# Three score banks, two woven sets of value banks, and two quarters moved into the last group of a two-layer decoder kernel

## The chip, the cores and the metric

The kernel runs on one core of a Trainium2 chip. The metric is the device time of one execution in microseconds; smaller is better. The core has TensorE (PE in the profile, its weight loads PEld), VectorE (DVE), ScalarE (ACT), GpSimd (POOL) and SyncE (SP), which issues nearly all DMAs. Matmul results go to PSUM, which has eight banks of 128 x 512 fp32 values; a bank can be written again when VectorE or ScalarE has read what was in it ("evicted" it).

## The reference

Two post-norm decoder layers over x of 4 x 256 tokens by 512, all in fp32: a latent attention with 32 heads, a gated feed-forward with integer weights, a causal attention with 32 heads, and a linear layer with soft-weighted low-rank experts.

```python
x = layernorm(x + L0_attn(x))
x = layernorm(x + L0_ffn(x))
x = layernorm(x + L1_attn(x))
x = layernorm(x + L1_ffn(x))

def L0_attn(h):                      # 32 heads, no mask
    q_c = h @ Wq_c.T + bq_c          # 192 wide
    q = (q_c @ Wq_up.T + bq_up)      # per head 128 + 64
    kv = h @ Wkv_c.T + bkv_c         # 64 latent + 64 shared key
    kvu = kv[..., :64] @ Wkv_up.T + bkv_up
    k = concat(kvu[..., :128], kv[..., 64:]);  v = kvu[..., 128:]
    o = softmax(q @ k.T / sqrt(192)) @ v
    return sum over heads of o @ Wo.T, + bo

def L1_attn(h):                      # 32 heads of 128, causal
    q = h @ wq;  k, v = split(h @ wkv)
    return softmax(mask(q @ k.T * 192 ** -0.5)) @ v @ wo
```

## The kernel before

The kernel is one program under a tile framework. The source gives instructions in an order, and a scheduler of the framework sets the order on each engine from it: an instruction may be put ahead of others of its engine. Each engine then works through its own list strictly in order and waits on semaphores. A `bank(tag)` is a PSUM tile of the pool that is open; the pool gives each tag so many banks, and a tile of a tag waits until the tile before it in the same bank has been read.

Stages, in order of time:

1. Projections and folding (0 to 56 us). `fold` folds key weights into query weights, in banks of the tag o.
2. The first attention (56 to 441 us), `NP` = 16 pairs of heads by `B` = 4 batches: 64 units. A unit computes the scores of two heads (`scores0`, L63 with output ps_s, one bank for each head), the maxima (L344), a bias (L348, L350), four exps on ScalarE (L355), the normalization (L364, L370 on VectorE, L368 on ScalarE), transposes (L379), their copies to SBUF (L383, one on each of VectorE and ScalarE), and the output (L396, bank o, copied by ScalarE, L400). In the loop the scores of a unit stand ahead of the transposes and the output of the unit before. Between them stand the queries of the next pair (`q_units`: `upper` L294, `lower` L302, evicted by ScalarE in L306) and, every other pair, a value product (`value_unit`), summed into `oacc` by VectorE (L409). GpSimd prepares weights of the second attention meanwhile (`prepare`, L136 to L139), which SP writes to DRAM.
3. The output projection: for each of eight token tiles a matmul with `wo0` in a bank p, VectorE's addition to x (L476), a layernorm, four transposes and a copy into `xT` (L128). A layernorm has two forms: by VectorE (L112 to L121, ScalarE does the square root) or, with `scalar`, by ScalarE with short VectorE steps between (L96 to L109).
4. The feed-forward (461 to 668 us), with products in the seven-product scheme (each 2 x 2 block product is made of seven products and sums of them). Its last loop does layernorm and transposes too.
5. The second attention. The eight groups of four heads (`NG`, `GH`) get queries and keys, and pairs of groups their values, by the seven-product scheme twice, an outer and an inner one. `seven` returns seven units of work; a unit is a product into one of three banks b0, b1, b2 and its eviction: by ScalarE (L792) or by VectorE as a sum (L795). The fifth and the last product go to the same bank.
   - The value stage (668 to 853 us): 28 stages of seven units, one after another in the order of `vorder`. Each stage asks for the weights of the third one behind it (`Stored.get`, DMAs qb and qc). After the first stage `input_blocks2` transposes the last two token tiles and makes combinations of the input on VectorE (`xcomb` L764, `blocks2` L523 to L526) and GpSimd; later stages need them.
   - Queries and keys of group 0 (853 to 880 us), then for each group 16 iterations of attention (four heads by four batches: `scores1` L63, L1084, L1088, L1092; `softmax1` L1104; `transposes1` L1110, L1112; `output1` L1119, L1120, written to DRAM as attd by SP). Between the parts of an iteration stand units of the next group's queries and keys, spread evenly by weight (`todo`). These consist of four stages each; the last, p = 3, has one inner product for each unit instead of two, and its result is added to heads 2 and 3 of the group (L879 on GpSimd). Partial products of stages with p = 1 and 3 lie in x[4:8], those of p = 2 in x[0:4], while x itself is in DRAM (`xd`).
   - In the last group's iterations there are no further queries; the units are those of the output projection of groups 0 and 1 (`stages_o`, L1043, 1052), and `lead` = 4 holds them back from the first and the last iterations. For them, behind the first iteration, SP loads attd (`o_load`, 2 MB each, into the buffers of old values and of old input combinations), the weights and x.
6. The output projection of groups 2 to 7 (1478 to 1616 us), and the expert layer (to 1706 us).

SP handles its list in order; a load that waits holds back those behind it. The end of each iteration's attention is written from three buffers `att`.

## Time and profile before

| | us |
|---|---|
| three timed runs | 1712.03, 1713.04 (median), 1717.1 |
| profiled execution | 1707.83 |
| its span, first to last instruction | 1706.0 |
| mean granted clock of TensorE | 0.998 |

| stage | from, to (us) | busy TensorE, VectorE, ScalarE, GpSimd |
|---|---|---|
| first attention, first units | 56, 126 | 70.0, 48.9, 42.9, 61.4 |
| first attention, the rest | 126, 438 | 300.2, 224.2, 195.3, 214.2 |
| its end and the projection | 438, 472 | 31.7, 24.5, 19.8, 13.2 |
| value stage, first four stages | 668, 702 | 28.9, 25.5, 6.1, 29.4 |
| value stage, the rest | 702, 853 | 150.6, 102.5, 28.7, 106.3 |
| second attention to its last group | 880, 1393 | 513.0, 358.3, 282.4, 375.2 |
| the last group's beginning | 1393, 1426 | 27.8, 23.8, 13.6, 28.3 |

Some records of matmuls are missing from a trace (some per cent), so that a small gap in TensorE's busy time need not be a wait; the waits by name and the distance from one start to the next tell more. A line such as `308.54 0.70 PE L63 MATMUL ps_s<-kT,qh ... x2` gives the start, the length, the engine, the line of the source, output and inputs, and how many records are merged. An fp32 matmul of the source is two records. In square brackets stands idle time of the engine before the row and what ended it.

### The profile page before, as it was taken

How to read it: one execution, taken by the hardware profiler on the slowest of the kernel's cores; microseconds unless marked ns; L12 is line 12 of the kernel's file. 1: busy time of each engine (PE TensorE's matmuls, PEld its weight loads, DVE VectorE, ACT ScalarE, POOL GpSimd, SP SyncE). 2: the span in 40 equal slices, each digit the busy share in tenths (PEclk: the TensorE clock that was granted, in tenths of full speed). 3: DMA queues.
4: the chain of work that ended last, by engine and by line, in shares of the span. 5: the costliest groups of instructions: out<-in, count | busy, mean ns of one | idle time of the engine just before them, and what ended most of it. 6: DMA issues, size and time to landing. Idle time of an engine off the chain costs nothing.

```text
span 1706.0 us, 24182 instructions
## 1 busy us (share of the span) xinstructions
PE 1662.6 (97%) x7954; PEld 1292.4 (76%) x7954; DVE 1066.8 (63%) x2351; ACT 701.4 (41%) x2066; POOL 1106.5 (65%) x1330
## 2 busy tenths in 40 slices
PE   8999999999999999999999999999999999999998
PEld 5566656666488888788878888888888878888854
DVE  3567777776754546676677666766667676433454
ACT  1566666656622101111115555555555562300043
POOL 1988878880236462876668668687686767689530
PEclk9999999999999999999999999999999999999999
DMA  9455555450222002567633233253332344443000
GB/s 339 152 208 202 205 216 209 174 190 36 69 70 73 27 25 72 179 228 246 205 97 123 102 110 135 75 178 113 100 134 75 117 160 171 158 149 116 33 19 31
DMA packets 96252, 226.90 MB, mean 133 GB/s; under 512 B 10272, under 2 KB 53792, under 8 KB 90112
## 3 DMA queue, kind: packets, MB, share of 16 engines
q1 hardware_dynamic: 94464, 224.54, 38.3%
q8 instruction: 64, 1.05, 0.3%
q10 hardware_dynamic: 1664, 0.81, 0.2%
q14 instruction: 60, 0.49, 0.1%
HBM read 140.38 MB, written 84.93 MB: 132 GB/s over the span
## 4 chain that ended last, share of the span: by engine, by line
PE 83%; DVE 10%; ACT 5%; issue 1%; DMA 1%; POOL 0%; DVEq 0%; ACTq 0%; POOLq 0%
PE ps_b L858 20%; PE ps_b L1043 11%; PE ps_b L953 10%; PE ps_s L63 9%; PE ps_o L1119 4%; ACT pr L355 3%; PE ps_s L604 3%; PE ps_p L294 3%; PE ps_o L63 2%; PE ps_p L63 2%; PE ps_t L1110 2%; PE ps_o L604 2%; PE ps_p L604 2%; PE ps_o L396 2%; DVE nmx L344 2%; DVE pr L370 2%
## 5 line engine op out<-in xcount | busy, mean ns | idle before, releaser
L1092 ACT ACTIVATE pr<-ps_s,nmx 128x128 f32<-128x128 f32 (+1 forms) x256 | 105.3, 418 | 106.2 <-DVE nmx L1088 106.2
L63 PE MATMUL ps_s<-kT,qh 128*128 128x256 f32 x512 | 130.5, 392 | 5.0 <-ACT pr L355 4.8
L1052 DVE TENSOR_TENSOR x<-ps_b,x 128x512 f32<-128x512 f32 x96 | 66.0, 690 | 108.5 <-PE ps_b L1043 101.2
L355 ACT ACTIVATE pr<-ps_s,ebias 128x256 f32<-128x256 f32 x256 | 117.9, 473 | 32.8 <-DVE ebias L350 30.8
L1104 ACT ACTIVATE pr<-pr,rc 128x128 f32<-128x128 f32 (+1 forms) x256 | 103.6, 448 | 61.3 <-DVE rc L1102 59.3
L63 PEld LDWEIGHTS ps_s<-kT,qh 128*128 128x128 f32 x512 | 90.9, 189 | 48.8 <-ACT pr L355 29.4
L1084 DVE TENSOR_TENSOR ps_s<-ps_s,mask 128x256 f32<-128x256 f32 x128 | 55.3, 432 | 108.3 <-PE ps_s L63 108.3
L795 DVE SCALAR_TENSOR_TENSOR x<-ps_b,p 128x512 f32<-128x512 f32 (+1 forms) x174 | 106.7, 614 | 25.1 <-PE ps_b L858 14.8
L792 ACT ACTIVATE p<-ps_b 128x512 f32<-128x512 f32 x92 | 51.5, 560 | 132.5 <-PE ps_b L953 76.0
L344 DVE TENSOR_REDUCE nmx<-ps_s 128x2 f32<-128x512 f32 x128 | 86.4, 686 | 27.4 <-PE ps_s L63 26.6
L136 POOL TENSOR_TENSOR ws<-ws 128x128 f32<-128x128 f32 (+1 forms) x128 | 70.7, 569 | 46.4 <-DMA ws<-in_wq 26.0
L370 DVE TENSOR_SCALAR pr<-pr,rc 128x256 f32<-128x256 f32 x192 | 93.4, 513 | 4.3
L1062 POOL TENSOR_TENSOR x<-x,po 128x512 f32<-128x512 f32 x48 | 60.1, 1271 | 38.1 <-DVE x L1052 29.6
L795 DVE SCALAR_TENSOR_TENSOR x<-ps_b,x 128x512 f32<-128x512 f32 (+1 forms) x116 | 71.1, 613 | 21.1 <-PE ps_b L953 12.1
L1119 PE MATMUL ps_o<-pT,v 128*128 128x256 f32 x256 | 82.9, 406 | 0.3 <-DVE pT L1112 0.2
L1088 DVE TENSOR_REDUCE nmx<-ps_s 128x1 f32<-128x128 f32 (+1 forms) x256 | 79.3, 351 | 3.7
L383 ACT COPY pT<-ps_t 128x512 f32<-128x512 f32 x64 | 37.5, 587 | 105.3 <-PE ps_t L379 105.3
L1112 DVE COPY pT<-ps_t 128x384 f32<-128x384 f32 x128 | 70.3, 550 | 11.5 <-PE ps_t L1110 11.5
L379 PE MATMUL ps_t<-ident,pr 128*128 128x128 f32 x512 | 70.0, 274 | 3.3 <-DVE pr L370 2.1
L139 POOL TENSOR_TENSOR ws<-ws,ws 128x128 f32<-128x128 f32 (+1 forms) x128 | 70.6, 566 | 2.4
L137 POOL TENSOR_TENSOR ws<-ws 128x128 f32<-128x128 f32 (+1 forms) x128 | 71.0, 571 | 1.3
L138 POOL TENSOR_TENSOR ws<-ws 128x128 f32<-128x128 f32 (+1 forms) x128 | 70.8, 567 | 1.3
(663 smaller groups left out, 4599.4 us busy)
## 6 DMA issues: line engine op xcount, KB each, us to landing
attd<-att SPq DMA_DIRECT2D x128, 128.0 KB, 1.8
vw<-ws SPq DMA_DIRECT2D x56, 256.0 KB, 2.4
qd<-ws SPq DMA_DIRECT2D x56, 256.0 KB, 2.3
qb<-vw SPq DMA_DIRECT2D x28, 512.0 KB, 4.6
qb<-qd SPq DMA_DIRECT2D x24, 512.0 KB, 4.5
v<-vd SPq DMA_DIRECT2D x6, 2048.0 KB, 8.6
qc<-vw SPq DMA_DIRECT2D x28, 384.0 KB, 4.1
vw<-ws SPq DMA_DIRECT2D x24, 384.0 KB, 2.4
```

What stands on the lines that cost most here:

```text
L63: nc.tensor.matmul(o, l, r, start=(i == 0), stop=(i == len(pairs) - 1))
L344: nc.vector.tensor_reduce(nmx[:, i, :], sc, AX.X, ALU.max, negate=True)
L355: nc.scalar.activation(pr[:, i, qt, :], sc[:, qt, :], AF.Exp, bias=bias[:, i, qt:qt + 1], accum_out=sm[:, i, qt:qt + 1],)
L370: nc.vector.tensor_scalar(prs, prs, rc[:, i, qt:qt + 1], None, ALU.mult)
L604: nc.tensor.matmul(banks_of[tag], lhs[i][:, k, :], rhs[i][:, k, :], start=first and k == 0, stop=k == 1, skip_group_check=True,)
L795: nc.vector.scalar_tensor_tensor(o[key], acc, scale, o[other], ALU.mult, ALU.add)
L858: nc.tensor.matmul(acc[:, e, :], pr.inner[i][k], inner[i][k], start=first and e == 0, stop=True, skip_group_check=True,)
L953: nc.tensor.matmul(acc[:, t, :].rearrange("p (h c) -> p h c", h=2), inner[i][k][:, t * P:(t + 1) * P], pr.inner[i][k], start=first and t = ...
L1043: nc.tensor.matmul(st[tag][:, tt, :], box["left"][i][:, k, (t0 + tt) * P:(t0 + tt + 1) * P], box["right"][i][:, k, :], start=first and tt ...
L1092: nc.scalar.activation(pr[:, pt, :], sc[:, pt, :], AF.Exp, bias=nmx[:, qt:qt + 1], accum_out=sm[:, qt:qt + 1],)
L1104: nc.scalar.activation(pr[:, pt, :], pr[:, pt, :], AF.Copy, scale=rc[:, qt:qt + 1])
L1119: nc.tensor.matmul(po, v[g][:, 2 * b, hv], pT[:, 0:2, :], start=True, stop=False)
```

## The change

- The first attention gets three score banks and one output bank instead of two and two; `fold` uses the score banks. Before the output projection the PSUM pool is closed and one with two banks of each of p, s, t, o is opened, which serves the feed-forward as before.
- In the feed-forward's last loop the layernorm of tile 6 takes the form on ScalarE, and the copies of the transposed tiles move from VectorE to ScalarE.
- The value stages alternate between the banks b0, b1, b2 and the banks s, t, o, and `woven` swaps the last unit of each stage with the first of the next. `input_blocks2` stands behind the second stage's first unit.
- The last quarter (p = 3) of the queries and of the keys of group 7 leaves the units of group 6's iterations; these 14 units come first in the last group's iterations, ahead of the output projection, and `lead` goes.
- For that the weights of the even output projections go to free slots of heads, those of the odd ones to the buffer w (it was the other way round), and x[4:8] is loaded when the first output stage begins, x[0:4] behind the first iteration as before.

```diff
-    ps0.enter_context(banks("ps0", p=2, s=2, t=2, o=2))
+    ps0.enter_context(banks("ps0", p=2, s=3, t=2, o=1))
...
         def fold(g):
-            pja = bank("o", (P, GH, RKV + 1))
+            pja = bank("s", (P, GH, RKV + 1))
...
-            pjb = bank("o", (P, GH // 2, RKV + 1))
+            pjb = bank("s", (P, GH // 2, RKV + 1))
...
+        ps0.close()
+        ps0.enter_context(banks("psf", p=2, s=2, t=2, o=2))
         for t in range(NT):
             pj = bank("p")
             mm(pj, [(oacc[:, t * P:(t + 1) * P], wo0)])
...
-                    layernorm(t)
+                    layernorm(t, t == NT - 2)
...
-                        turned(t - 2)
+                        turned(t - 2, nc.scalar.copy)
...
+        def woven(units):
+
+            flat = [u for us in units for u in us]
+            for n in range(1, len(units)):
+                k = sum(len(us) for us in units[:n])
+                flat[k - 1], flat[k] = flat[k], flat[k - 1]
+            return flat
...
-            stages[0]["w"] = lambda: pr.load(odd if r % 2 else False)
+            stages[0]["w"] = lambda: pr.load(False if r % 2 else even)
...
-            groups.append([*sq, *sk])
+            if g == NG - 1:
+
+                groups.append([*sq[:3], *sk[:3]])
+                rest = [sq[3], sk[3]]
+            else:
+                groups.append([*sq, *sk])
...
+        def back(t0):
+
+            for t in (t0, t0 + 2):
+                nc.sync.dma_start(out=x[:, t:t + 2, :], in_=xd[:, t:t + 2, :])
+
+        so[0][0]["load"] = lambda: back(4)
+
         first[0]()
-        for n, (g, p) in enumerate(vorder):
...
-            for u, _ in values[g][p]:
+
+        vunits = [values[g](p, ("s", "t", "o") if n % 2 else ("b0", "b1", "b2")) for n, (g, p) in enumerate(vorder)]
+        for n, us in enumerate(vunits):
+            def begin(n=n, u=us[0]):
+                if n + 3 < len(vorder):
+                    later = vorder[n + 3]
+                    pv[later[0]].get(later[1])
...
                 u()
-            if n == 0:
-                input_blocks2()
+                if n == 1:
+                    input_blocks2()
+
+            us[0] = begin
+        for u in woven(vunits):
+            u()
...
-            units = units_of(so[0] + so[1]) if last else units_of(groups[g + 1])
-            total, at, todo, lead = sum(w for _, w in units), 0, {}, 4 if last else 0
+            units = units_of(rest + so[0] + so[1]) if last else units_of(groups[g + 1])
+            total, at, todo = sum(w for _, w in units), 0, {}
             for u, w in units:
-                todo.setdefault(lead + (2 * at + w) * (4 * GH * B - 2 * lead) // (4 * total), []).append(u)
+                todo.setdefault((2 * at + w) * 4 * GH * B // (4 * total), []).append(u)
...
-                    odd.extend((free.pop(0), free.pop(0)))
+                    even.extend((free.pop(0), free.pop(0)))
...
-                    for t0 in (0, 2):
-                        for t in (t0, t0 + 4):
-                            nc.sync.dma_start(out=x[:, t:t + 2, :], in_=xd[:, t:t + 2, :])
+                    back(0)
```

## The prediction

> **What bounds the kernel now.** First the page's busy times, then the stretches, then the matmuls in order of time. Part 1 names TensorE:
>
> ```profile
> span 1706.0 us, 24182 instructions
> PE 1662.6 (97%) x7954; PEld 1292.4 (76%) x7954; DVE 1066.8 (63%) x2351; ACT 701.4 (41%) x2066; POOL 1106.5 (65%) x1330
> ```
>
> At most 43 us are idle there, and a busy PE is not PE at its peak, so I measure lost time by starts. Back to back, a 128x256 record starts 0.2155 us after the one before, a 128x128 0.109, a 128x512 0.43 (most common distances in the timeline). The stretches that the change touches, by the busy times of each engine (PE, PEld, DVE, ACT, POOL, clock, DMA):
>
> ```profile
> 56.00:126.00 70.00, 70.00 (x328) 45.72 (x328) 48.86 (x119) 42.86 (x139) 61.41 (x120) 1.00 0.59 212
> 126.00:438.00 312.00, 300.23 (x1485) 193.73 (x1484) 224.19 (x528) 195.28 (x614) 214.19 (x400) 1.00 0.47 170
> 438.00:472.00 34.00, 31.72 (x113) 14.21 (x112) 24.50 (x66) 19.84 (x48) 13.20 (x16) 1.00 0.35 106
> 668.00:702.00 34.00, 28.87 (x120) 22.36 (x121) 25.54 (x37) 6.06 (x11) 29.44 (x35) 0.95 0.32 105
> 702.00:853.00 151.00, 150.61 (x674) 125.35 (x673) 102.47 (x148) 28.67 (x48) 106.28 (x77) 1.00 0.67 233
> 880.00:1393.00 513.00, 513.00 (x2685) 442.53 (x2684) 358.31 (x864) 282.43 (x902) 375.15 (x437) 1.00 0.34 109
> 1393.00:1426.00 33.00, 27.81 (x137) 21.36 (x136) 23.75 (x46) 13.63 (x50) 28.33 (x17) 1.00 0.64 248
> ```
>
> They are the first attention (two rows), its output projection, the start of the value stage, the rest of it, the second attention up to its last group, and that group's start. TensorE is full in the second attention; what can be won lies in the others. The waits of TensorE put names to it (total, times, longest):
>
> ```profile
> PE ps_s L63 <- ACT pr L355: 4.8, 9, 1.4
> PE ps_b L953 <- DVE vb L795: 3.5, 2, 2.7
> PE ps_b L1043 <- DMA att<-attd: 2.5, 1, 2.5
> PE ps_t L379 <- DVE pr L370: 2.1, 4, 0.9
> ```
>
> **The change part by part**, with the built order of each engine's instructions beside the timeline. No arithmetic is added or removed; one layernorm and six copies of the second layernorm's transposes move from VectorE to ScalarE; banks and orders change.
>
> *Order in the first attention.* In the first eight units (60.43 to 107.90) the old order puts one lower query product (L302) in every unit; in all later units, and in all units of the new order, two stand together. Two units with split products take 72.30 - 60.43 = 11.87 us; two undisturbed ones with the products together take 308.54 - 297.79 = 10.75, since the two 64-row products then run side by side:
>
> ```profile
> 63.23 1.23 PE L302 MATMUL ps_p<-qcT,wmb 64*128 64x512 f32 x2
> 306.36 1.23 PE L302 MATMUL ps_p<-qcT,wmb 64*128 64x512 f32 x4
> ```
>
> Two records take as long as four. Four pairs of units: 4 x 1.12 = 4.5 us; I take 4, since the unevenly filled units may wait some tenths on the softmax. Bounds 1.5 to 4.5.
>
> *Third score bank.* It removes at most the waits on L355, 4.8 us, and with them follow-up waits of the transposes on the normalization (2.1 by DVE, 0.6 by ACT): 0 to 8. Only one head's scores can run ahead, and the softmax chain itself is slowed where GpSimd works (L370's pair 1.77 us at 231.40, 0.62 at 440.51), which no bank mends. I take 3.5. The single output bank costs nothing: ScalarE's order has the copy that empties it (L400) ahead of the copy (L383) that the next output waits for.
>
> *The end of the first attention.* New banks are opened before the output projection. In the new order the projection's first matmul stands behind the last value product and waits for the last sum into oacc (L409); in the old one four projections ran inside the last two units. VectorE has 16.0 us of work here: 8 x 0.687 (L476), 5 x 1.74 (layernorm: 0.68 + 0.17 + 0.14 + 0.16 + 0.59), 3 x 0.6. It began at 441.4 and ended at 458.7; in the new order, from the same exps, the last transposes, output, value product and sum end near 446.5. From 5.1 go the 1.9 us of attention work that stood inside the old stretch, and 1.0 to 1.7 come on top, since three of the last chunk's first products now stand behind the last transposes instead of one. Cost +4, bounds 0 (the chain overlaps after all) to +8.
>
> *Value stage, steady part.* Each stage is seven products of four records, 6.03 us. The old ones take 758.81 - 752.58 = 6.23, as the last product of each waits for the bank that the fifth left, and the next stage for another:
>
> ```profile
> 756.90 1.03 PE L953 MATMUL ps_b<-qc,xT 128*128 128x256 f32 x4
> 757.84 1.13 PE L953 MATMUL ps_b<-qb,x 128*128 128x256 f32 x4
> 758.81 1.03 PE L953 MATMUL ps_b<-qb,t 128*128 128x256 f32 x4
> ```
>
> 0.94 and 0.97 instead of 0.862. Weaving puts a product of the other set between. The 24 stages from 702.07 to 853.08 lose 151.0 - 24 x 6.03 = 6.3 us, nearly all of this kind; VectorE has 102 of 151 us to do, so it follows. I take -5.5, bounds -3 to -6.3. The weights' loads are asked for one product earlier and land 4.1 to 4.6 us after issue against two stages: hidden.
>
> *Value stage, start.* Four stages and eight transposes take 702.07 - 668.16 = 33.9 us instead of 25.0. VectorE makes input blocks in one piece (L764, L523 to L526) of 1.3 + 8 x 0.67 + 1.5 = 8.2 us, and old banks fill up behind it:
>
> ```profile
> 682.29 0.67 DVE L523 TENSOR_TENSOR x<-xT 128x256 f32<-128x256 f32 x1
> 689.17 3.06 PE L953 MATMUL ps_b<-qb,x 128*128 128x256 f32 x8 [2.71 <-DVE vb L795]
> ```
>
> In the new order this piece still stands whole, behind the second stage's first sum. Stepping through with 0.862 a product and 0.69 a sum: TensorE stops 2.3 us at the second stage's fifth product, then runs five products of other banks, stops 3.7 us at its sixth, and has 28 products near 700.0, not 702.07. The moved layernorm and copies don't bring the start forward: the second copy now stands on ScalarE behind the square root of tile 7, +0.4. I take -2, bounds +1 to -8.
>
> The granted clock was 0.95 over this stretch, half for 3.4 us after the 2.71 us wait: 1.7 us of work. A stop of 3.7 us would bring such a halving again, so none of it is counted as won.
>
> The Trainium skill (TensorE: Matmul & The Clock Gate, "HAM oscillation") warns of idle gaps over some 3.4 us, after which the clock is halved. By it the 3.7 us stop, and any such gap at the projection, cost up to 1.7 us each more than a steady clock; behind its first 11 us this trace has one halving inside the work, and the rule would make my sum about 2 us smaller if two were added.
>
> *Last group.* The last quarters of queries and keys (14 units of two records, 6.03 us) leave the stretch before, which is full, and go where TensorE waits for attd:
>
> ```profile
> 1391.23 1.27 POOL L879 TENSOR_TENSOR slot_(False, 31)_11850<-slot_(False, 29)_11848,x 128x512 f32<-128x512 f32 x1
> 1395.23 0.32 SPq L1213 DMA_DIRECT2D x<-xd  x1
> 1397.08 0.56 SPq L1006 DMA_DIRECT2D att<-attd  x1
> 1408.55 1.97 PE L1043 MATMUL ps_b<-w,att 128*128 128x256 f32 x8 [2.46 <-DMA att<-attd]
> ```
>
> From 1393.1 to 1426 TensorE loses 9.1 us. In the new order the att load stands on SP behind both loads of x[0:4], which wait for six sums on GpSimd (6 x 1.27 = 7.6 us after the last full quarter). So it starts near 8 and lands, with 1 MB of x ahead, near 17.5, against 15.3 + 6.0 = 21.3 on the same count: 3.8 us won. x[4:8] comes behind w and xo, near 25; TensorE needs its sum near 28, but VectorE may stand some 4 us before it, with the attention's maxima behind. I take -3, bounds +2 to -7.
>
> **Sum:** -4 - 3.5 + 4 - 5.5 - 2 - 3 = -14 us. The profiled execution took 1707.83 us (span 1706.0), 5 below the median 1713.04 of the three timed ones; taking the difference over to the median gives **1699 us**.
>
> **The rivals.**
> (a) *The first attention is paced by the softmax loop*, not by TensorE: VectorE has 224 of 312 us there, but bias, exps, scaling and maxima follow one another, 0.3 + 1.8 + 0.5 + 1.3 us, then copy and transposes: about 5 to 5.9 a unit, as long as TensorE's 5.4. Then pairing gives 1.5 and the bank nothing: -8, 1705 us. Against it: undisturbed units at 4.98.
> (b) *VectorE is not late at the value start and the projection overlaps*: -5 and -4 more, 1690 us. For it: the six banks; against: VectorE's block stands whole.
> (c) *The last stretch gives its gain back*: sums on GpSimd or x[4:8] late, VectorE stands before x. +2 instead of -3: 1704 us.
> (d) *Slower: the projection becomes a chain, tile by tile.* One tile alone is 1.06 + 0.69 + 1.74 + 0.5 (ScalarE's root and hand-overs) + 0.64 + 0.57 = 5.2 us; eight are 41.6 instead of VectorE's 16. That adds 25: +11, 1724 us. It decides from 14 us more than I charge. For it: TensorE's order holds 20 transposes in a row; against: VectorE's order has projections of later tiles ahead of each layernorm.
> (e) *It doesn't do what it says*: the third bank and the second set stand empty because the sums come late anyway: 1713 us.
>
> **How the numbers follow.** Forecast 0.47 (own range 1693 to 1706), (a) 0.14, (b) 0.14, (c) 0.10, (d) 0.06, (e) 0.09. The range 1688 to 1709 takes in (a), (b), (c) and leaves out most of (d) and (e). A measurement of this kernel tells 0.3%, about 5 us, from no change: faster 0.79, same 0.14, slower 0.07.
>
> **What would show it.** The chain's share of L355 falls and no wait of ps_s on ACT is left over 1 us; unit pairs at 60 to 108 take 10.8; value stages take 6.03 to 6.08; the last tile's transposes of the projection come 3 to 6 us later after the last exp; the att load starts 2 to 4 us after the quarter's last matmul, TensorE's loss before L1043 shrinks. Wrong if value stages stay at 6.2, if the projection overlaps, or if VectorE stands before x in the last group.

## The result and the profile after

The changed kernel took 1705.28 us in the median of six runs (1702.05 to 1707.48), the kernel before 1713.37 (six runs, 1709.53 to 1717.1): ratio 0.995, 95% interval 0.9931 to 0.9969. That is 8 us faster, where 14 were forecast. The profiled execution took 1705.43 us (span 1703.4), only 2.4 less than that of before (1707.83), because the profiled execution of before was quicker than every one of its timed runs.

The two traces cut into the same stages, by the start of the first record named (us):

| mark | before | after | difference |
|---|---|---|---|
| first scores of the first attention (L63) | 55.07 | 52.30 | -2.8 |
| last scores of the first attention | 437.25 | 437.31 | +0.1 |
| first feed-forward product with combined weights (c0wg) | 472.71 | 478.40 | +5.7 |
| first value product | 668.16 | 673.98 | +5.8 |
| first query product of group 0 | 853.09 | 856.61 | +3.5 |
| last transposes of the second attention | 1476.52 | 1473.88 | -2.6 |

The last column adds up from the start of the program. So the first attention began 2.8 us earlier and lost it again in its loop; the output projection cost 5.6; the value stage gained 2.3 instead of 7.5; the second attention gained 6.2 instead of 3. The busy times by stretch (TensorE, its weight loads, VectorE, ScalarE, GpSimd, clock, DMA share, GB/s):

```profile
126.00:437.00 311.00, 298.07 (x1470) 192.28 (x1469) 223.98 (x521) 192.89 (x608) 213.72 (x400) 1.00 0.47 170
437.00:478.00 41.00, 34.99 (x125) 15.79 (x124) 27.89 (x69) 20.28 (x50) 16.89 (x20) 1.00 0.35 106
674.00:707.00 33.00, 29.21 (x137) 24.98 (x138) 27.16 (x37) 6.35 (x11) 28.93 (x35) 1.00 0.33 106
707.00:857.00 150.00, 145.18 (x659) 125.73 (x658) 103.74 (x144) 28.11 (x47) 107.49 (x78) 0.99 0.72 235
1393.00:1426.00 33.00, 29.97 (x154) 25.21 (x153) 22.04 (x46) 13.82 (x46) 25.75 (x16) 1.00 0.64 249
```

The first attention is no fuller than before: 298.07 of 311 us against 300.23 of 312. The value stage, which had been full behind its first four stages, has a hole of 4.8 us. In the waits of TensorE (us in total, times, longest) the wait that the third bank was to remove, ps_s on L355, is gone. Three others of the first attention have grown in its place (first, second and fourth line); the third and the last line are of the value stage:

```profile
PE ps_p L63 <- ACT qh L306: 6.2, 11, 1.0
PE ps_t L379 <- DVE pr L370: 4.6, 7, 0.9
PE ps_s L963 <- DMA qb<-vw: 4.6, 1, 4.6
PE ps_t L379 <- ACT pr L368: 3.7, 6, 0.7
PE ps_o L963 <- DVE vb L797: 2.5, 1, 2.5
```

Before, the first line stood at 2.5 us, the second at 2.1, the wait on L368 at 0.6, and L355 at 4.8: 10.0 us in all, now 14.5. Two lines of before:

```profile
PE ps_p L63 <- ACT qh L306: 2.5, 8, 0.4
PE ps_t L379 <- ACT pr L368: 0.6, 4, 0.2
```

*The first attention.* ScalarE's timeline shows where the wait on L368 comes from. Two evictions of queries and a copy stand ahead of the scaling, and TensorE's last transposes wait for it:

```profile
138.33 1.28 ACT L306 ACTIVATE qh<-ps_p,qb 128x512 f32<-128x512 f32 x2
139.47 0.40 ACT L400 COPY pc<-ps_o 128x256 f32<-128x256 f32 x1
139.72 0.55 ACT L368 ACTIVATE pr<-pr,rc 128x256 f32<-128x256 f32 x1
...
140.33 0.55 PE L379 MATMUL ps_t<-ident,pr 128*128 128x128 f32 x3 [0.69 <-ACT pr L368]
```

*The output projection.* The last transposes end near 464.7 and not 460.7. Of the feed-forward's first products (f0wg) three stood in gaps between the transposes before (the last rows there):

```profile
460.25 0.60 PE L127 MATMUL ps_t<-ident,x 128*128 128x128 f32 x4
460.68 1.02 PE L63 MATMUL ps_p<-xT,f0wg 128*96 128x512 f32 x2
```

After the change only one does, and the others follow in one row:

```profile
462.44 0.65 PE L127 MATMUL ps_t<-ident,x 128*128 128x128 f32 x4 [1.09 <-ACT xT L128]
462.93 1.02 PE L63 MATMUL ps_p<-xT,f0wg 128*96 128x512 f32 x2
463.79 1.04 PE L127 MATMUL ps_t<-ident,x 128*128 128x128 f32 x8
464.66 2.74 PE L63 MATMUL ps_p<-xT,f0wg 128*96 128x512 f32 x6
```

*The value stage.* Its products run without the old hand-over from 715 on (6.04 us a stage). But at the sixth stage TensorE stands still for a load of weights, and then runs at half clock (2.07 us for what takes 1.03):

```profile
707.85 1.03 PE L963 MATMUL ps_b<-qc,t 128*128 128x256 f32 x4
713.44 2.07 PE L963 MATMUL ps_s<-qb,xT 128*128 128x256 f32 x4 [4.56 <-DMA qb<-vw]
715.30 1.82 PE L963 MATMUL ps_b<-qb,x 128*128 128x256 f32 x4
```

SP's queue shows that the load was issued directly behind a store of values; it then needs 5.0 us to land, at 713.39 (the median of such loads is 4.5):

```profile
698.47 0.32 SPq L498 DMA_DIRECT2D qc<-vw  x1
708.00 0.32 SPq L956 DMA_DIRECT2D vd<-vb  x1
708.41 0.38 SPq L498 DMA_DIRECT2D qb<-vw  x1
```

The store waits for GpSimd's sum, which ends at 707.97. GpSimd began at 677.84 with 17 us of combinations of the key weights of group 0, whose queries and keys begin only at 856.61, then made the input blocks, and only then came to the sums:

```profile
677.84 1.27 POOL L136 TENSOR_TENSOR c<-w 128x512 f32<-128x512 f32 x1 [17.20 <-PE ps_b L963]
...
694.33 0.45 POOL L139 TENSOR_TENSOR cc<-c,cc 128x128 f32<-128x128 f32 x1
694.75 0.73 POOL L525 TENSOR_TENSOR x<-xT 128x256 f32<-128x256 f32 x1
...
703.80 4.17 POOL L950 TENSOR_TENSOR vb<-vb 128x512 f32<-128x512 f32 x3
```

The same row of work stood there before, and in both traces GpSimd ends these sums 34 us after the first value product (668.16 before). But TensorE came to the sixth stage's first product 40 us after it before, and would come 34.7 us after it now: the load was just in time, and is late. Before:

```profile
698.24 3.73 POOL L940 TENSOR_TENSOR vb<-vb 128x512 f32<-128x512 f32 x3
708.49 1.03 PE L953 MATMUL ps_b<-qb,xT 128*128 128x256 f32 x4
```

*The last group.* The load of att goes out 8.2 us behind the last full quarter (its last matmul ends at 1387.8) and 2.9 us behind the moved quarter of the queries (1393.0). With less ahead of it and beside it, it lands 8.2 us after its issue instead of 11.3, and the first product that needs it starts at 1404.30 instead of 1408.55:

```profile
1395.95 0.38 SPq L1016 DMA_DIRECT2D att<-attd  x1
```

From 1385 to 1480 TensorE's distances from start to start exceed those of an undisturbed row by 5.2 us in all; before it was 9.6.

### The profile page after: what moved, and what is told of

The parts are those of the page before. It is cut to its first block, busy times and chain, and to the rows that moved or that the text cites. A ratio compares the mean times of both kernels' runs of the same rounds, so it can differ in the third digit from the quotient of the medians.

```text
span 1703.4 us, 24156 instructions
## 1 busy us (share of the span) xinstructions
PE 1652.0 (97%) x7954; PEld 1293.3 (76%) x7954; DVE 1071.0 (63%) x2344; ACT 708.4 (42%) x2077; POOL 1105.6 (65%) x1330
## 4 chain that ended last, share of the span: by engine, by line
PE 79%; DVE 10%; ACT 6%; POOL 2%; issue 1%; DMA 1%; SPq 0%; DVEq 0%; POOLq 0%; ACTq 0%
PE ps_b L868 20%; PE ps_b L1053 11%; PE ps_s L63 9%; PE ps_b L963 4%; PE ps_o L1129 4%; ACT pr L355 4%; PE ps_s L606 3%; PE ps_p L63 3%; PE ps_t L1120 2%; PE ps_p L294 2%; DVE pr L370 2%; DVE nmx L344 2%; PE ps_o L606 2%; PE ps_p L606 2%; PE ps_o L63 2%; PE ps_t L963 2%
## 5 line engine op out<-in xcount | busy, mean ns | idle before, releaser
L355 ACT ACTIVATE pr<-ps_s,ebias 128x256 f32<-128x256 f32 x256 | 118.0, 474 | 36.3 <-DVE ebias L350 33.9
L63 PE MATMUL ps_s<-kT,qh 128*128 128x256 f32 x512 | 131.4, 393 | 0.1
L63 PEld LDWEIGHTS ps_s<-kT,qh 128*128 128x128 f32 x512 | 91.4, 189 | 42.1 <-issue 30.9
L1094 DVE TENSOR_TENSOR ps_s<-ps_s,mask 128x256 f32<-128x256 f32 x128 | 55.3, 432 | 106.8 <-PE ps_s L63 106.8
L797 DVE SCALAR_TENSOR_TENSOR x<-ps_b,p 128x512 f32<-128x512 f32 (+1 forms) x159 | 96.5, 607 | 21.8 <-PE ps_b L868 13.0
L136 POOL TENSOR_TENSOR ws<-ws 128x128 f32<-128x128 f32 (+1 forms) x128 | 70.7, 568 | 43.8 <-DMA ws<-in_wq 24.6
L370 DVE TENSOR_SCALAR pr<-pr,rc 128x256 f32<-128x256 f32 x192 | 96.2, 528 | 4.4
L379 PE MATMUL ps_t<-ident,pr 128*128 128x128 f32 x512 | 73.5, 276 | 8.9 <-DVE pr L370 4.6
L379 PEld LDWEIGHTS ps_t<-ident,pr 128*128 128x128 f32 x512 | 59.1, 141 | 24.7 <-ACT pr L368 6.4
L1122 DVE COPY pT<-ps_t 128x384 f32<-128x384 f32 x128 | 70.5, 551 | 10.6 <-PE ps_t L1120 10.2
L794 ACT ACTIVATE p<-ps_b 128x512 f32<-128x512 f32 (+1 forms) x78 | 43.2, 554 | 75.2 <-PE ps_b L868 43.7
L797 DVE SCALAR_TENSOR_TENSOR x<-ps_b,x 128x512 f32<-128x512 f32 (+1 forms) x106 | 64.3, 608 | 15.3 <-PE ps_b L868 8.7
L396 PE MATMUL ps_o<-pT,cN 128*64 128x256 f32 x512 | 71.5, 392 | 0.4 <-DVE pT L383 0.2
## 6 DMA issues: line engine op xcount, KB each, us to landing
qc<-vw SPq DMA_DIRECT2D x28, 384.0 KB, 3.7
vw<-ws SPq DMA_DIRECT2D x24, 384.0 KB, 2.4
```

Source lines behind the costliest of these rows:

```text
L63: nc.tensor.matmul(o, l, r, start=(i == 0), stop=(i == len(pairs) - 1))
L355: nc.scalar.activation(pr[:, i, qt, :], sc[:, qt, :], AF.Exp, bias=bias[:, i, qt:qt + 1], accum_out=sm[:, i, qt:qt + 1],)
L370: nc.vector.tensor_scalar(prs, prs, rc[:, i, qt:qt + 1], None, ALU.mult)
L379: nc.tensor.transpose(tp[:, kt, qt * P:(qt + 1) * P], pr[:, i, qt, kt * P:(kt + 1) * P], ident)
L797: nc.vector.scalar_tensor_tensor(o[key], acc, scale, o[other], ALU.mult, ALU.add)
```

## The experiments

Each ratio is to the kernel before, run on the same chip at the same time, with its 95% interval. "First to last scores" is the length of the first attention's loop; "projection" the way from the last scores to the first product with c0wg (35.5 us before, 41.1 after); "value stage" goes from its first product to group 0's first query product.

### The three parts alone

`first_alone` is the kernel before with the first point of the change alone: the banks of the first attention, fold in the score banks, and new banks opened before the output projection.

> The kernel before with the first attention's part alone: three score banks and one output bank, fold in the score banks, new banks opened before the output projection. Theory S (the softmax loop paces the first attention, so that a bank more and the pairing of the lower query products bring nothing): the last scores stand at 436 to 438 us of the span as before (437.3), the way from there to the feed-forward's first product on split weights grows from 34.6 to 39 to 41 us, and the whole is slower by 4 to 7 us: 1717 to 1720. Theory F (the forecast's terms of -4 and -3.5 hold, and something else in the changed kernel ate them): last scores at 429 to 433 us, the whole faster by 1 to 4 us.

Measured: 1714.85 us against 1711.85, ratio 1.0014 (0.9994 to 1.0035). First scores at 51.66, last at 439.27, projection 41.2. The first attention's part alone makes nothing faster: it starts 3.4 us earlier, its loop gives that back, and the projection costs 5.7. Theory S holds in direction. Its last scores (436 to 438) came later, and the whole is 3.0 us slower by the medians and not 4 to 7; the earlier start, which S had left out, would account for that, but no run parts it from the loop's scatter (table below).

`value_alone` is the kernel before with the woven value stages and the moved layernorm and copies.

> The kernel before with the value stage's part alone: two sets of banks, woven, with the layernorm of tile 6 and the copies on ScalarE. Theory L (the quicker start runs into a load of weights that stands on SP behind a store of values, which waits for GpSimd's sums): one product near the sixth stage waits 3 to 5 us for qb, the value stage takes 182 to 184 us instead of 184.9, later stages 6.03 to 6.06 each, the whole is faster by 1 to 3 us. Theory F (the load is late only in the changed kernel, where the projection shifted everything): no such wait, the value stage takes 176.5 to 179 us and the whole is faster by 6 to 8 us.

Measured: 1708.32 us against 1711.85, ratio 0.9969 (0.995 to 0.9989); value stage 182.49 us. Theory L, by the wait and the stage's length: the late load needs nothing of the other parts. The whole, 3.5 us faster by the medians, is a little better than L said.

```profile
716.79 0.32 SPq L954 DMA_DIRECT2D vd<-vb  x1
717.20 0.38 SPq L496 DMA_DIRECT2D qb<-vw  x1
```

Again the load stands behind the store, and TensorE waited 4.5 us for it.

`last_alone` is the kernel before with the new places of the last quarters, the weights and x.

> The kernel before with the last group's part alone: the last quarters of queries and keys of group 7 in the last group's iterations, x and weights loaded in the new places. If the gain there is the last group's own (theory own): TensorE loses 4.5 to 5.5 us from 1385 to 1480 instead of 9.6, query start to the last attention transpose takes 616.5 to 618.5 us instead of 623.4, the whole is faster by 4 to 7 us. If part of it came with the value stage's new banks or with where things landed (theory elsewhere): 620 to 621.5 us, faster by 2 to 3 us (the forecast's term was 3).

Measured: query start to last attention transposes 617.07 us, loss from 1385 to 1480 4.5 us: by the trace the gain is the last group's own, 6.4 us. The timed ratio is weaker, 0.9991 (0.9967 to 1.0014), since the runs of this kernel scatter from 1702.56 to 1718.26. In the profiled one the first attention, which the edit doesn't touch, took 387.5 us from first to last scores instead of 382.2.

### Where the projection's cost comes from

`late_switch` is the changed kernel with the opening of new banks moved:

```diff
-        ps0.close()
-        ps0.enter_context(banks("psf", p=2, s=2, t=2, o=2))
         for t in range(NT):
...
             turned(t, nc.scalar.copy)
+        ps0.close()
+        ps0.enter_context(banks("psf", p=2, s=2, t=2, o=2))
```

> The changed kernel with the new PSUM banks opened behind the output projection instead of before it. Theory P (opening new banks keeps the projection's products behind the attention's last value product): from the last scores to the feed-forward's first product on split weights 33.5 to 35.5 us instead of 40.2, the whole 4.5 to 6.5 us faster than the changed kernel's 1705.3: 1699 to 1701. Theory E (the first attention with one output bank ends with a longer chain in any case): 38.5 to 40.5 us, 1704 to 1706.

Measured: 1706.3 us, ratio 0.9963 (0.9942 to 0.9984), projection 42.75 us: neither theory. The projections overlap the attention's end again (the first at 439.73, last transposes done near 460.4), but now the feed-forward's first products stand behind the opening, the gaps between the transposes stay empty, and the clock falls to half:

```profile
452.00:458.00 6.00, 2.79 (x16) 1.72 (x15) 4.96 (x20) 4.73 (x13) 1.18 (x2) 0.87 0.54 156
458.00:464.00 6.00, 5.23 (x15) 2.93 (x14) 1.77 (x2) 1.76 (x3) 4.79 (x7) 0.50 0.87 298
```

TensorE is busy 2.79 of 6 us in the first row; in the second the granted clock is 0.50, and the first eight records of f0wg (four products), 3.4 us at full clock, take 6.2.

`one_pool` opens nothing in between: the third score bank has a tag of its own, and tags go round.

```diff
+        if tag in rota:
+            count[tag] = n = count.get(tag, -1) + 1
+            tag = rota[tag][n % len(rota[tag])]
...
-    ps0.enter_context(banks("ps0", p=2, s=3, t=2, o=1))
+    ps0.enter_context(banks("ps0", p=2, s=2, t=2, o=1, u=1))
+    rota["s"] = "ssu"
...
-        ps0.close()
-        ps0.enter_context(banks("psf", p=2, s=2, t=2, o=2))
+        rota.clear()
+        rota["o"] = "ou"
```

> The changed kernel with one PSUM pool from the first attention to the end of the feed-forward: the third score bank has a tag of its own (u), scores go round s, s, u, and the feed-forward's output products go round o, u. Nothing is closed and opened before or behind the projection. Theory P (whatever stands first behind the opening of new banks waits, the projection in the changed kernel, the feed-forward's first products where the opening stands behind the projection): from the last scores to the feed-forward's first product on split weights 34 to 36.5 us instead of 41.1 (counted to c0wg), the whole 4 to 6 us faster than the changed kernel: 1699 to 1702 on the same chip scale. Theory E (the one output bank and the order at the loop's end are the cost): 39 to 42 us, no gain.

Measured: 1700.99 us, ratio 0.9929 (0.9905 to 0.9954); projection 36.53 us. Theory P: the opening of new banks cost 4.6 of the 5.6 us. The other 1.1 go with the three score banks and the single output bank: `two_banks` (below), also one pool but with two and two, takes 35.46 us as before, and `scale_first`, the same kernel with the changed banks, 36.53. The value stage here still waits 4.3 us for qb and takes 181.70 us, so that the one pool alone doesn't mend it.

### What the late load waits for

`wk_hold` is the changed kernel with the key weights' load held back:

```diff
-        first[0]()
+        hold = l1.tile([P, DC, GH * DN], F32, tag="w", name="hold", bufs=1)
+        nc.gpsimd.memset(hold[:, 0, :1], 0.0)
...
+                if n == 8:
+                    nc.vector.tensor_tensor(hold[:, 0, :1], hold[:, 0, :1], lastp[0][:, 0, :1], ALU.add)
+                    first[0]()
```

> The changed kernel with the load of group 0's key weights held until the ninth value stage (its buffer is first written and read by two tiny operations), so that GpSimd's 17 us of combinations of them no longer stand ahead of the value stage's first sums. Theory Q (the late load of qb stands on SP behind a store of values, and that behind GpSimd): the store goes out 6 to 12 us earlier, no product of the value stage waits over 1 us for qb, the value stage takes 175.5 to 178 us instead of 182.6, the whole 4 to 7 us faster than the changed kernel: 1698 to 1701. Theory R (the load is late for another reason, its buffer or the DMA queues): the wait for qb stays at 3 us or more.

Measured: 1711.23 us, ratio 0.9998 (0.9977 to 1.0018). The old wait is gone and stages 4 to 10 take 6.04 to 6.05 us each. But the value stage takes 186.8 us: at the first products of the twelfth and the thirteenth stage, with GpSimd at those combinations from 723.71 on, the same wait comes back twice:

```profile
743.01 2.08 PE L966 MATMUL ps_s<-qb,t 128*128 128x256 f32 x4 [3.04 <-DMA qb<-vw]
...
754.97 2.05 PE L966 MATMUL ps_b<-qb,xT 128*128 128x256 f32 x4 [4.13 <-DMA qb<-vw]
```

Theory Q names the mechanism rightly (what holds GpSimd up holds the store, and the store the next load), and its forecast of the time fails, since the 17 us only moved.

`loads_on_act` leaves GpSimd's order alone and takes the loads out of SP's queue; it also has the one pool.

```diff
-                    pv[later[0]].get(later[1])
+                    pv[later[0]].get(later[1], nc.scalar)
```

> The changed kernel with one PSUM pool (third score bank u) as before, and the value stage's loads of weights issued from ScalarE's queue instead of SP's, so that no store of values stands ahead of a load. Theory Q (the late load is SP's order behind a store that waits for GpSimd): no wait for qb over 0.5 us, stages behind the fourth take 6.04 to 6.4 us, the value stage 175.5 to 178 us; with the one pool's 36.5 us at the projection the whole is 9 to 12 us faster than the changed kernel would be, about 0.988 to 0.990 of the kernel before. Theory N (the wait goes on to the next holder: ScalarE's copies stand behind loads that wait for buffers, or for blocks that GpSimd frees late): the value stage stays at 180 us or more.

Measured: 1693.79 us, ratio 0.9882 (0.9856 to 0.9908), projection 36.52, value stage 177.53 us. No wait for qb is left. Theory Q.

```profile
699.10 0.33 ACTq L504 DMA_DIRECT2D qc<-vw  x1
700.01 0.60 ACT L801 ACTIVATE p<-ps_b 128x512 f32<-128x512 f32 x1 [2.90 <-PE ps_b L970]
700.82 0.33 ACTq L504 DMA_DIRECT2D qb<-vw  x1
```

ScalarE issues the loads between its copies, and its idle time in this row ends with TensorE, not with a load's buffer.

### What paces the first attention

`quiet_before` and `quiet_after` are the kernels before and after without GpSimd's inner combinations of stored weights; the later stages of both work on other numbers.

```diff
-                    inner_left(outer[i], thirds(c[:, e]))
...
-                nc.sync.dma_start(out=dc[:, 2 * p:2 * p + len(pair)], in_=c[:, :len(pair)])
+                    nc.sync.dma_start(out=dc[:, 2 * p + e, 0:2], in_=outer[i][:, 0].rearrange("p (n c) -> p n c", n=2))
+                    nc.sync.dma_start(out=dc[:, 2 * p + e, 2], in_=outer[i][:, 1, :DN])
```

> The kernel before without GpSimd's inner combinations of the second attention's stored weights (the stored pieces are copies of the outer combinations instead, so later stages work on other weights; shapes and amounts of DMA stay nearly the same). In the first attention GpSimd loses about four fifths of its work. Theory G (GpSimd stretches VectorE's short operations and thereby the softmax loop): the mean of L370 falls from 0.52 to 0.36 to 0.42 us, TensorE's named idle time from 60 to 430 us falls from 11 to 18 us to under 6, first to last scores take 373 to 379 us instead of 382 to 395. Theory C (the chain of bias, exps, scaling and copies is too long by itself): L370 falls, but idle time stays over 9 us and the loop over 381.

> The changed kernel without the same combinations on GpSimd (same replacement). Theory G: first to last scores take 369 to 374 us instead of 384 to 388, that is 4 to 5 us less than the kernel before without them: the third bank and the paired products bring what was forecast only where GpSimd leaves VectorE alone. Theory C: the loop stays over 380 us, with waits of the transposes on L368 and L370.

Measured, one execution each (1711.93 and 1698.74 us): first to last scores 385.5 and 380.1 us. The mean of L370 is 0.48 us in both, not 0.36 to 0.42: fewer scalings meet GpSimd, but those that do meet its long operations (1.3 us), and in the quiet changed kernel 29 of 160 between 110 and 430 us take 1.04 us in the mean. TensorE's idle time between its records from 60 to 430 us is 12.2 and 10.6 us (10.9 and 15.1 with all of GpSimd's work). Theory G fails as it was put, and Theory C gets its idle time and its loop (the second by 0.1 us). In the quiet changed kernel the waits on L306 and L368 fall to 1.6 and 1.3 us, while that on L370 grows to 7.1 (11 times). The runs don't settle how much of the loop is GpSimd's: other executions with all of its work took 380 us too (table below).

`q_on_dve` and `scale_first` are `loads_on_act` with ScalarE's row ahead of the transposes shortened in two ways.

```diff
+                    if n:
+                        nc.vector.tensor_scalar(
+                            qh[h][:, cols], acc[n], QSCALE, qb[:, h:h + 1], ALU.mult, ALU.add
+                        )
+                        continue
```

> The same as the kernel with loads on ScalarE, and in the first attention the second head's queries are evicted by VectorE instead of ScalarE (one of two each, 0.64 us). Theory A (the third bank moved the loop's wait to ScalarE, where two query evictions of 1.28 us stand ahead of the scaling L368 that the transposes wait for): the named waits of transposes on L368 fall from 3 to 4 us to under 1.5, those of value products on the evictions from 5 to 6 to under 3, first to last scores take 374 to 380 us instead of 380 to 388. Theory V (VectorE, whose short operations GpSimd stretches, is as much the pace as ScalarE): waits move to L370, the loop stays at 380 to 388.

Measured: 1699.97 us, ratio 0.9919 (0.9887 to 0.9951), no better than `loads_on_act`; loop 383.7 us. Theory V: the wait on L368 is gone, and VectorE has taken its place:

```profile
PE ps_t L390 <- DVE pr L381: 5.9, 8, 1.0
PE ps_p L68 <- DVE qh L313: 5.9, 10, 1.0
```

L381 and L313 are this kernel's scaling and query eviction on VectorE.

```diff
+                softmax0(pr, sm)
                 if todo:
                     todo.pop(0)()
...
-                pending = (j, b, softmax0(pr, sm))
+                pending = (j, b, pr)
```

> The same as the kernel with loads on ScalarE, and in the first attention the source gives the scaling of a unit's probabilities ahead of the query products and the output of the unit before; ScalarE's order becomes eviction, scaling, eviction, copy instead of eviction, eviction, copy, scaling. Theory A: the transposes' waits on L368 nearly vanish (under 1 us), first to last scores take 374 to 380 us. Theory V: waits on L370 and on bank p grow instead, the loop stays at 380 to 388.

Measured: 1689.64 us, ratio 0.9861 (0.9833 to 0.9889); loop 377.1 us; no wait on ScalarE's scaling is listed, and that on VectorE's is 3.8 us (4.4 in `loads_on_act`). Theory A, by ScalarE's wait and the loop, in one profiled execution; the value products' wait on L312 stays at 6.0 us. This is the fastest version here: 22 us under the kernel before. Its lead over `loads_on_act`, about 4 us, is within the intervals, but the trace shows its mechanism, the scaling (here L374) now between the two evictions (L312):

```profile
136.74 0.70 ACT L312 ACTIVATE qh<-ps_p,qb 128x512 f32<-128x512 f32 x1
137.31 0.52 ACT L374 ACTIVATE pr<-pr,rc 128x256 f32<-128x256 f32 x1
137.71 0.70 ACT L312 ACTIVATE qh<-ps_p,qb 128x512 f32<-128x512 f32 x1
```

`two_banks` is `scale_first` with two score and two output banks in the first attention, as before the change.

> The kernel with loads on ScalarE and the scaling first, but with two score banks and two output banks in the first attention as in the kernel before (fold in the output banks, one pool without u). Theory W (the third score bank is worth its forecast 3.5 us or more once ScalarE's order doesn't hold the transposes back): first to last scores take 381 to 386 us against 377.1 with three banks, waits of the scores on L355 come back with 4 to 8 us, the whole is 3 to 8 us slower than the three-bank kernel's 0.986: 0.988 to 0.991 of the kernel before. Theory Z (the softmax chain paces, the number of score banks does not matter): 375 to 380 us, 0.984 to 0.987.

Measured: 1692.89 us, ratio 0.9869 (0.9832 to 0.9906). The waits on L355 are back (8.1 us, 14 times), as W has it, but the time cannot be told from that with three banks. The profiled execution can't decide either: in its second unit VectorE stood for some 6 us (the last section), and its loop took 394 us. From the thirteenth unit on, behind the stop, two banks took 312.3 us and the three of `scale_first` 306.3, which is W's way; but the six executions with three banks in the changed kernel's order scatter from 308.5 to 316.0 us over the same units. The two ratios differ by 0.0008 (1.4 us), far less than their intervals; what the third bank is worth by itself stays open.

The loop over all executions profiled with all of GpSimd's work:

| score banks | first scores at (us) | first to last scores (us) |
|---|---|---|
| two: before, `last_alone` | 55.07, 55.04 | 382.2, 387.5 |
| two, with VectorE's stop: `value_alone`, `two_banks` (the latter in the order of `scale_first`) | 55.02, 55.27 | 395.2, 394.1 |
| three: after, `first_alone`, `late_switch`, `wk_hold`, `loads_on_act` | 52.30, 51.66, 51.78, 51.57, 51.20 | 385.0, 387.6, 384.0, 380.0, 385.5 |
| three, with VectorE's stop: `one_pool` | 52.48 | 389.9 |
| three, other order: `q_on_dve`, `scale_first` | 53.35, 52.29 | 383.7, 377.1 |

Without the stop, two banks take 384.8 us in the mean of two executions and three in the changed kernel's order 384.4 in the mean of five: the same, in a scatter of some 4 us to each side. The 377.1 of `scale_first` lies below all others.

## Why the prediction held, and where its steps failed

The direction was right, and 1705.3 us lies in the range of 1688 to 1709, 6 us above the value named. The terms, with what the traces gave for each:

| term | forecast | measured |
|---|---|---|
| order of L302, third score bank | -4 - 3.5 | start -2.8, loop +2.8; over the executions listed above start -1.7 to -3.9, loop 0 within some 4 |
| end of the first attention | +4 | +5.6 |
| value stage, first four stages | -2 | -4.4 |
| value stage, the rest | -5.5 | +2.1: -4.4 as in `loads_on_act`, and +6.5 by the late load |
| last group | -3 | -6.2 |
| sum | -14 | -2.6 in the two profiled executions, -8.1 by the medians |

The 5.5 us between the two sums stand in no term. The first attention's loop of before is a likely place: it took 382.2 us in the trace that the forecast was read from, and 387.5 in `last_alone`, whose first attention is the same.

*The first attention, order and bank: failed.* Pairing is worth what was said where nothing waits: the two units from 82.78 to 93.53 took 10.75 us. The eight units from 64.36 to 110.37 took 46.0 instead of 47.5 for the old first eight, not 43. And the bank removed the wait on L355 as forecast, all 4.8 us of it; the term's mistake is the step that with it the waits of the transposes go too. They grew, from 2.1 and 0.6 to 4.6 and 3.7 us, with the scaling on ScalarE behind the query evictions and on VectorE among operations that GpSimd stretches. This is rival (a), which had a chance of 0.14; `q_on_dve`, where the wait only changed its engine, and `scale_first`, where ScalarE's went and the loop shortened, speak for it, with one trace each. What the working had not seen is the earlier start, some 3 us. It comes with fold in the three score banks: all kernels with them start between 50.9 and 53.4, all with fold in the two output banks between 53.7 and 55.3. Whether the number of banks or their place does it, no run tells.

*The end of the first attention: right in mechanism, sized too small.* The working had 5.1 - 1.9 = 3.2 us for the last transposes and 1.0 to 1.7 for products that lose their gaps, 4.2 to 4.9, and took 4. The last transposes come 4.0 us later (3.3 counted from the last exp), and two of the feed-forward's first products (0.86 us each) stand behind them, 1.7 us. `late_switch` and `one_pool` show that 4.6 us of the cost belong to opening banks, wherever that stands; the other 1.1 go with the banks' numbers, so "The single output bank costs nothing" does not hold at the loop's end. Rival (d) didn't happen.

*The value stage: the steady part right, "hidden" wrong.* Stages take 6.04 us, within the 6.03 to 6.08 named, but a few take 6.38 and the last 6.57, so that without the late load the 24 gain 4.4 us and not 5.5. The first four came out better than stepped through (stops of 1.4 and 2.7 us instead of 2.3 and 3.7, and no halving there). The step that failed is "The weights' loads are asked for one product earlier and land 4.1 to 4.6 us after issue against two stages: hidden". It took the load's time and not its place: in SP's queue it stands behind a store, the store behind GpSimd, and GpSimd behind 17 us of foreign work. With the loads on another queue the stage takes 175.6 to 177.5 us, 7.4 to 9.4 less than before: the -7.5 was there to be had.

*The last group: right, sized too small.* The att load was issued 8.2 us behind the last full quarter ("near 8") and landed 16.4 behind it ("near 17.5"). In the traces' own times it was issued 1.1 us earlier and landed 4.3 us earlier, although this attention began 3.5 us later. VectorE did not stand before x[4:8], and TensorE lost 4.4 us less from 1385 to 1480 (3.8 of it was worked out, 3 taken); the other 1.8 us lie in the stretches before, which the forecast had called full. The -3 allowed for a late x[4:8] (rival (c)), which did not come late.

That rival (a)'s 1705 is the time measured is partly chance, and so is that the forecast came within 6 us: the late load (6.5 us) was in neither, and the larger gain in the last group (3 us) and the earlier start (3 us) made up for it. The sign that the chain's share of L355 would fall was wrong: it rose from 3% to 4%. Rival (b)'s six banks at the value start brought half of what (b) said, and its overlapping projection didn't come.

## What to carry to other kernels

Before a load is called hidden, follow its queue back: to the store ahead of it, to the engine that this store waits for, and to what that engine does first; a faster start of one engine doesn't pull such a chain forward. Opening a new PSUM pool held back what stood first behind it in both places tried here; when only one bank changes its use, let tags go round in one pool. A further buffer helps only as far as the next wait in order, so look at what stands ahead of that wait's releaser on its engine, and change that order along with the buffer.

## What the runs showed of the hardware

*VectorE held by GpSimd.* From 110 to 430 us in the changed kernel's trace, the 42 scalings L370 that GpSimd's work overlaps by less than half took 0.35 us each, 0.355 at most; the other 114 took 0.60 us in the mean and up to 1.42. The Trainium skill (SBUF — State Buffer, "Who interferes with whom") says that the two share a port pair as a lock, and that the one that issues second blocks until the other's instruction has finished: the longest, 1.42 us, is less than 0.35 and one of GpSimd's 1.27 together, which agrees. But in three executions of fourteen VectorE stood far longer, each time in the loop's first units, here in `one_pool` for an operation on four columns:

```profile
58.09 8.76 DVE L354 TENSOR_TENSOR nmb<-nmx,beta 128x4 f32<-128x4 f32 x1
```

GpSimd ran a gapless row of instructions of some 0.45 us (rows of two in 0.86 us, the last in 1.67) from before 58 to 66.8 us, so VectorE stood through some seventeen of them, not one; that they held it is read from the two engines' times alone. The clock then fell to 0.70 from 66 to 76 us; in `value_alone` and `two_banks` a scaling of 6.59 us in the same place cost a 4.6 us stop of TensorE and a clock of 0.58 and 0.60 over the same stretch. These stops are a part of the scatter of this kernel's runs.

*The clock.* The Trainium skill (TensorE: Matmul & The Clock Gate, "HAM oscillation") puts the halving behind idle gaps of some 3.4 us. Here the 4.56 us wait was followed by it, and so was every stop of TensorE of more than 4 us inside the first attention and the value stage of the fourteen traces. But the stop of 2.95 us at the value start halved the clock in `loads_on_act` and left it alone in `scale_first`:

```profile
690.20 1.55 PE L970 MATMUL ps_t<-qb,x 128*128 128x256 f32 x4 [2.95 <-DVE vb L804]
691.54 1.06 PE L970 MATMUL ps_o<-qb,x 128*128 128x256 f32 x2
692.40 1.91 PE L970 MATMUL ps_b<-qc,x 128*128 128x256 f32 x4
```

```profile
684.63 1.13 PE L971 MATMUL ps_t<-qb,x 128*128 128x256 f32 x4 [2.95 <-DVE vb L805]
685.60 0.59 PE L971 MATMUL ps_o<-qb,x 128*128 128x256 f32 x2
686.03 1.03 PE L971 MATMUL ps_b<-qc,x 128*128 128x256 f32 x4
```

And in `late_switch` it was 0.50 behind stops of 0.86, 1.78 and 1.44 us with little work between them. A stop of 3.04 us in `wk_hold` was followed by the halving and one of 3.28 us was not; one of 2.10 us in the feed-forward was followed by it in `value_alone` and not in the kernel before. So the page's figure is no safe lower bound here: under some 3.3 us it depends on more than the gap's length. Every slow stretch inside the work of these traces lasted 3.41, 6.83 or 10.24 us, which is once, twice or three times the same time.
